# Pooling the second level of keys and values after the projection, on GpSimd, instead of before it

## The chip, the cores and the metric

The kernel runs on one core of a Trainium2 chip. Its engines work side by side, each through its own queue in order: TensorE (PE, with its weight loads as PEld), VectorE (DVE), ScalarE (ACT), GpSimd (POOL), and SyncE (SP), which issues transfers. The metric is device microseconds of one execution. The kernel before takes 3242.17 us, the median of 3 runs from 3239.64 to 3243.61.

## What is computed

The input is `x`, 8 images of 256 channels by 32x32. Three parts follow one another: a pooled attention with a depthwise convolution (layer 0), a self-attention over 1024 positions, and a mixture of 8 experts. The change lies in layer 0 alone, in its keys and values:

```python
kv = jnp.einsum('bchw,oc->bohw', x, kv_w)
k_map, v_map = (kv[:, :C], kv[:, C:])

def pooled(t):
    outs = []
    for i, r in enumerate(POOL_RATIOS):              # [1, 2, 3, 6]
        oh, ow = (round(H / r), round(W / r))        # 32, 16, 11, 5
        Mh, Mw = (_pool_mat(H, oh), _pool_mat(W, ow))
        p = jnp.einsum('bchw,ph,qw->bcpq', t, Mh, Mw)
        p = p + _depthwise(p, dconv_w[i], dconv_b[i])
        outs.append(p.reshape(B, C, -1))
    return jnp.concatenate(outs, axis=2)
```

So the keys and the values each have 1024 + 256 + 121 + 25 = 1426 positions per image: the projected map itself, its means over 2x2 blocks (the second level, 16x16), over blocks of about 3x3 (11x11) and of about 6x6 (5x5), each with a 3x3 depthwise convolution added. Layer norm, scores, softmax and the weighted sum of the values follow. Projection and pooling are both linear, so either may come first.

## The kernel before, in words

`kernel` builds one program. A guarded general version (`layer0_general` and others) follows at its end and runs only if a bound is broken. What is timed is `attention` (layers 0 and 1a, line 913) and `experts`, both written as generators that a planner, `Flow` (line 657), puts into an order while the program is built. Each generator yields the engine that it needs and the tiles that must be ready; `Flow` keeps a clock per engine from modelled costs (`cost`, line 723), the time at which each tile is ready, and, for DVE and POOL, a shared port on which POOL operations and DVE operations with two SBUF inputs follow each other (line 795). Generators have a rank, lower first. `step` (line 882) runs whatever is due between two steps of the main loop, as far as a credit of PE time allows (4.0 us a step for ranks below 5, 2.0 for the others, lines 29 to 31); `finish` runs generators until a condition holds. Every engine's instructions then keep this order on the chip.

**The main loop** (line 1911) goes over 8 batches (images), with 45 steps each: `scores` of one chunk of 128 keys against 512 queries of four heads (four matmuls, then one exp of 128x2048 on ACT, line 1512), and `values` of the chunk before. Pairs of exps are added by accumulating transfers from POOL's queue (`add`, line 1567) and then on DVE (`sums`, line 1574). One PSUM tile `sc` serves all scores, and six `pt` tiles hold the exps.

**Beside it**, for each later batch, `prepare` (line 1381) loads and normalises the image `xi`; `pool_levels` (line 1332) sums its 2x2, 3x3 and 6x6 blocks into `xl`, 402 columns: level 2 on POOL (add neighbouring columns, add neighbouring rows, scale by a quarter), level 3 on POOL, level 4 on DVE. `maps` (line 1114) projects four maps, two channel halves of values (m = 2, 3) and two of keys (m = 0, 1), in the column slices `KEY_SLICES` = 512, 512, 402, the last from `xl`. ACT copies each slice from PSUM to the map `p`, and writes `acc`, the slice times (1 + middle tap) plus the bias, for the levels in that slice. `convolve` (line 1273) adds the eight other taps per level on DVE (`taps`, line 1245), level by level, in `todo`'s order; two buffers `p` and three buffers `acc` limit how far maps run ahead. `by_tokens` turns the result to tokens, normalises it, and `key_tokens` writes the keys `kn`. Once a batch is done with layer 0, the self-attention (`layer1`, `outputs`) of that batch runs in the same gaps of the main loop.

**Batch 0** has its own path, since nothing runs beside it: `first_maps` (line 1173) projects the four maps in another order, and the large level of its keys is convolved on PE with diagonal weights (`first_keys`); `first_taps` does the rest on DVE. The small levels of its two key maps go to a tile `ptail`.

PE's matmuls of 128x128 weights are cut into four column quarters of 32 within the main loop (`Flow.Engine`, line 677), which run beside one another. One fp32 matmul leaves two records in the trace for each piece.

Of the kernel before, what the change touches and what calls it, by code (L numbers as in the profile page):

```python
# [42 lines left out]
LIMIT = 1e12  # L43
KEY_CHUNKS = [(i * P, min(P, NK - i * P)) for i in range(NKC)]
KEY_SLICES = [(0, 512), (512, 512), (1024, 402)]


K_ID, K_GRP, K_ONE, K_S11, K_S5, K_HEAD, K_I32, K_SEL, K_END = 0, 128, 256, 384, 505, 530, 658, 690, 706
# [864 lines left out]
def attention(tc, kit, f, outer, ended, nb, consts, x, t1, t2, hn, bounds, vecs, q_t, kv_t, proj_t, gqk_t, wqk, wqkv, vecs1, w1_d, w1c, gate_d, wrc, vecs2, bnvec):  # L913
# [6 lines left out]
    with ExitStack() as ctx:  # L920
# [50 lines left out]
        def db(c, s):  # L971
# [4 lines left out]
        f.ve.tensor_scalar(  # L976
            mid, vec[:, V_DW : V_DW + 72].rearrange("p (a t) -> p a t", t=9)[:, :, 4], 1.0, None, ALU.add
        )
        hi, lo = bounds
        for t in bounds:  # L980
            f.pool.memset(t, 0.0)
# [119 lines left out]
        def pool(*tiles):  # L1101
            return "POOL", tiles, None
# [4 lines left out]
        def until(cond):  # L1107
            return None, cond, None

        def source(xp, s0, w):  # L1110
            xi, xl = xp
            return xi[:, :, s0 : s0 + w] if s0 < HW else xl[:, :, s0 - HW : s0 - HW + w]

        def maps(xp):

            for m in (2, 3, 0, 1):
                c = m % 2
                yield until(
                    lambda: read[0] >= len(todo) - 1 and len(todo) < (3 + 2 * max(freed[0], 2) if freed[0] else 5)
                )  # L1120
                p = pmaps[len(todo) % 2]
                acc = T(work, [P, NK], "acc", bufs=3)
                for s0, w in KEY_SLICES:
                    if s0 >= HW:
                        yield until(lambda: len(done) >= len(todo) - 1)
                    src = source(xp, s0, w)
                    yield pe(src, tag="sm")
                    ps = small()
                    for k in range(2):
                        f.pe.matmul(  # L1130
                            ps[:, :w],
                            lhsT=kvw[:, k, m * P : (m + 1) * P],
                            rhs=src[:, k, :],
                            start=k == 0,
                            stop=k == 1,
                        )
                    f.act.activation(p[:, s0 : s0 + w], ps[:, :w], AF.Copy)
                    for s, n in enumerate(SIDES):
                        a, z = max(OFFS[s], s0), min(OFFS[s] + n * n, s0 + w)
                        if a < z:  # L1140
                            f.act.activation(
                                acc[:, a:z],
                                ps[:, a - s0 : z - s0],
                                AF.Identity,
                                bias=db(c, s),
                                scale=mid[:, c * 4 + s : c * 4 + s + 1],
                            )
                todo.append((c, p, acc))
# [7 lines left out]
        pmaps = [T(work, [P, NK], f"p{i}") for i in range(2)]  # L1156
        for t in pmaps:
            f.split(t, 512, HW)
        first, large, whole, pooled, asked = {}, [], [], [], []

        def first_diagonals():

# [10 lines left out]
        def first_maps(xp):  # L1173


            for m in range(4):
                if m < 2:
                    p = T(work, [P, 4, 512], "pt", bufs=6).rearrange("p j q -> p (j q)")
                    acc = T(l1, [P, NK], "v") if m else T(work, [P, NK], "kn", bufs=3)
                else:  # L1180
                    p = pmaps[m - 2]
                    acc = T(work, [P, NK], "acc", bufs=3)
                for t in (p, acc):
                    if t is not p or m < 2:
                        f.split(t, 512, HW)
                first[m] = p, acc
            for m, s0 in [(m, s0) for g in (0, 2) for s0 in (0, 512) for m in (g, g + 1)] + [(m, HW) for m in range(4)]:
                if s0 == HW:
                    yield until(lambda: pooled)
                w = min(512, NK - s0)  # L1190
                c = m % 2
                p, acc = first[m]
                src = source(xp, s0, w)
                yield pe(src, tag="sm")
                ps = small()
                for k in range(2):
                    f.pe.matmul(
                        ps[:, :w],
                        lhsT=kvw[:, k, m * P : (m + 1) * P],
                        rhs=src[:, k, :],  # L1200
                        start=k == 0,
                        stop=k == 1,
                    )
                small_levels = s0 == HW and m < 2
                f.act.activation(ptail[:, m, :w] if small_levels else p[:, s0 : s0 + w], ps[:, :w], AF.Copy)
                for s, n in enumerate(SIDES):
                    a, z = max(OFFS[s], s0), min(OFFS[s] + n * n, s0 + w)
                    if a < z and (m >= 2 or s):
                        f.act.activation(
                            acc[:, a:z],  # L1210
                            ps[:, a - s0 : z - s0],
                            AF.Identity,
                            bias=db(c, s),
                            scale=mid[:, c * 4 + s : c * 4 + s + 1],
                        )
                if (m, s0) == (3, 512):
                    large.append("maps")
                    f.spawn(first_keys(0), 1)
                    f.spawn(first_keys(1), 5)
            whole.append("maps")  # L1220
# [38 lines left out]
        def first_taps():  # L1259
            for m in (2, 3):  # L1260
                yield until(lambda: "maps" in large)
                yield from taps(m - 2, 0, *first[m])
                large.append(("values", m))
                read[0] += 1
            yield until(lambda: whole)
            for m in (0, 1, 2, 3):
                p, acc = first[m]
                for s in range(1, 4):
                    yield from taps(m % 2, s, *((ptail[:, m, :], acc, HW) if m < 2 else (p, acc)))
                whole.append(m)  # L1270
            done.extend(first[m][1] for m in (2, 3, 0, 1))

        def convolve():

            for m in range(4, 4 * nb):
                yield until(lambda: len(todo) > m)
                c, p, acc = todo[m]
                for s in range(4):
                    yield from taps(c, s, p, acc)
                    read[0] += s == 0  # L1280
                done.append(acc)
# [50 lines left out]
        def pool_levels(xi, xl):  # L1332
# [2 lines left out]

            def level(s):
                n = SIDES[s]
                return xl[:, :, OFFS[s] - HW : OFFS[s] - HW + n * n].rearrange("p k (h w) -> p k h w", h=n)

            for k in range(2):  # L1340
                one, l2, l3 = img[:, k], level(1)[:, k], level(2)[:, k]

                yield pool(xi)
                t2 = T(work, [P, 32, 16], "pool")
                f.pool.tensor_tensor(t2, one[:, :, 0::2], one[:, :, 1::2], ALU.add)
                yield pool(t2)
                f.pool.tensor_tensor(l2, t2[:, 0::2, :], t2[:, 1::2, :], ALU.add)
                yield pool(t2)
                f.pool.tensor_scalar(l2, l2, 0.25, 1.0, ALU.mult, ALU.mult)

                yield pool(xi)
                t3 = T(work, [P, 32, 11], "pool")
                f.pool.tensor_tensor(t3, one[:, :, 0::3], one[:, :, 1::3], ALU.add)
                yield pool(t3)
                f.pool.tensor_tensor(t3[:, :, 0:10], t3[:, :, 0:10], one[:, :, 2::3], ALU.add)
                yield pool(t3)
                f.pool.tensor_tensor(t3[:, :, 1:11], t3[:, :, 1:11], one[:, :, 2::3], ALU.add)
                yield pool(t3)
                f.pool.tensor_tensor(l3, t3[:, 0::3, :], t3[:, 1::3, :], ALU.add)
                f.pool.tensor_tensor(l3[:, 0:10, :], l3[:, 0:10, :], t3[:, 2::3, :], ALU.add)  # L1360
                yield pool(t3)
                f.pool.tensor_tensor(l3[:, 1:11, :], l3[:, 1:11, :], t3[:, 2::3, :], ALU.add)
                flat = xl[:, k, OFFS[2] - HW : OFFS[3] - HW]
                f.pool.tensor_tensor(flat, flat, con[:, K_S11 : K_S11 + 121], ALU.mult)

            t5 = T(work, [P, 2, 32, 5], "pool")
# [6 lines left out]
            for i, (a, e) in enumerate(ends):  # L1373
                f.ve.tensor_reduce(
                    l5[:, :, i, :], t5[:, :, a:e, :].rearrange("p k h w -> p k w h"), AX.X, ALU.add
                )
            flat = xl[:, :, OFFS[3] - HW :]
            f.ve.tensor_tensor(flat, flat, con[:, None, K_S5 : K_S5 + 25].to_broadcast([P, 2, 25]), ALU.mult)
            pooled.append(True)

        def prepare(b):
# [28 lines left out]
            for k in range(2):  # L1410
# [1 line left out]
                f.ve.tensor_scalar(  # L1412
                    xi[:, k, :], xi[:, k, :], mu[:, k : k + 1], gr[:, k : k + 1], ALU.subtract, ALU.mult
                )
            xl = T(work, [P, 2, NK - HW], "xl")
            if b == 0:
                f.spawn(pool_levels(xi, xl), 2)
            else:
# [1221 lines left out]
```

## Time and profile before

| | |
|---|---|
| median of 3 runs | 3242.17 us |
| the profiled execution | 3241.38 us |
| its span (first to last instruction) | 3239.2 us |
| busy: PE, DVE, ACT, POOL | 3072.6, 2403.2, 1690.1, 1201.7 us |
| mean granted PE clock | 0.985 |
| first scores of batches 0 to 7 | exps from 83, 307, 537, 764, 995, 1219, 1457, 1680 us |
| last exp of the main loop | 1866 us |
| projections of the last slice | 51.9 to 59 us (batch 0), 142 to 1496 us (the others) |
| DVE's taps | 960 instructions into `acc`, 550 us |

The page of a profile gives for each engine its busy time; the stages below it cut the span into windows. A row of a group of instructions reads: line, engine, operation, out<-in, shapes, count, then busy us and mean ns of one, then idle time of the engine just before them and what ended it. All instructions of the planner carry line 670, so groups are told apart by tile names: `sm` and `sx` are PSUM tiles for small work, `p`, `acc`, `xi`, `xl` and `pool` (the sums' scratch tile) are those above.

### The profile page before, as it was taken

The numbers are of one execution on the slowest core, as the hardware profiler recorded it, in microseconds if no ns is written. First come the engines' busy times: TensorE is split into PE (matmuls) and PEld (weight loads), VectorE is DVE, ScalarE is ACT, GpSimd is POOL, SyncE is SP. The second block draws the span as 40 slices with busy tenths as digits, with TensorE's granted clock in tenths as the row PEclk, the third lists the DMA queues.
The fourth block names the chain that finished last, engine by engine and source line by source line (L and its number), as shares of the span: only waits on it lengthen the run. The fifth ranks groups of instructions, "written<-read, shape, count | busy, mean of one in ns | idle before, by whom it ended". The sixth has DMA issues, their size and how long they took to land. (4 is left out here: it accounts for less than half of the span.)

```text
span 3239.2 us, 56567 instructions
## 1 busy us (share of the span) xinstructions
PE 3072.6 (95%) x22678; PEld 1788.4 (55%) x22678; DVE 2403.2 (74%) x4128; ACT 1690.1 (52%) x2302; POOL 1201.7 (37%) x1293
## 2 busy tenths in 40 slices
PE   8787899899999989999999999999999999999998
PEld 3322234343334333433433357777888888888887
DVE  5896888888888888788544545446878788877776
ACT  4675666666666576666655533333333333444443
POOL 2313213223232231321121220006756666777776
PEclk9898999999999999999999999999999999999999
DMA  1467665655656665655667763124344452000000
GB/s 54 93 145 160 123 140 128 145 131 126 160 122 119 158 132 106 163 120 122 145 135 144 156 213 127 59 85 169 140 153 144 148 170 72 20 24 29 20 14 21
DMA packets 117200, 375.54 MB, mean 116 GB/s; under 512 B 14512, under 2 KB 40440, under 8 KB 93696
## 3 DMA queue, kind: packets, MB, share of 16 engines
q0 software_dynamic: 28608, 179.85, 28.6%
q1 hardware_dynamic: 84960, 190.01, 17.3%
q8 instruction: 181, 2.97, 0.4%
q10 hardware_dynamic: 3360, 1.97, 0.2%
q14 instruction: 91, 0.75, 0.1%
HBM read 118.74 MB, written 87.60 MB: 64 GB/s over the span
## 5 line engine op out<-in xcount | busy, mean ns | idle before, releaser
L670 ACT ACTIVATE pt<-sc 128x2048 f32<-128x2048 f32 x352 | 660.7, 1877 | 271.2 <-PE sc L670 222.3
L670 DVE SCALAR_TENSOR_TENSOR acc<-p,vec,acc 128x961 f32<-128x961 f32 (+3 forms) x960 | 550.3, 582 | 31.6 <-ACT acc L670 6.1
L670 PE MATMUL sc<-q,kn 32*128 32x512 f32 (+1 forms) x3072 | 424.1, 653 | 98.5 <-ACT pt L670 94.8
L670 DVE TENSOR_TENSOR pt<-pt,pt 128x1024 f32<-128x1024 f32 x320 | 390.5, 1264 | 162.1 <-DMA pt<-pt 133.9
L670 PE MATMUL pv<-pt,vt 128*32 128x512 f32 x2816 | 388.8, 625 | 2.8 <-ACT vt L670 2.8
L670 ACT ACTIVATE p1c<-bank 128x256 f32<-128x256 f32 x226 | 86.4, 382 | 557.1 <-PE bank L670 545.4
L670 ACT ACTIVATE h<-h,bnvec 128x512 f32<-128x512 f32 x452 | 341.9, 805 | 61.8 <-DVE h L670 53.5
L670 POOL DMA_DIRECT2D pt<-pt x160 | 146.4, 915 | 568.4 <-ACT pt L670 435.1
L670 POOL TENSOR_TENSOR rstd<-rstd,mhalf 128x4 f32<-128x4 f32 (+2 forms) x88 | 102.7, 1168 | 614.4 <-DVE rstd L670 600.6
L670 DVE TENSOR_TENSOR h<-p1c,bank 128x512 f32<-128x512 f32 x226 | 153.9, 681 | 223.6 <-PE bank L670 216.8
L670 PEld LDWEIGHTS sc<-q,kn 32*128 32x128 f32 (+1 forms) x3072 | 114.4, 180 | 293.1 <-ACT pt L670 189.0
L670 POOL TENSOR_TENSOR tm<-h,tm 128x256 f32<-128x256 f32 x202 | 236.2, 1169 | 15.8
L670 DVE TENSOR_TENSOR h<-u,bank 128x256 f32<-128x256 f32 x452 | 230.0, 550 | 7.8
L670 PEld LDWEIGHTS pv<-pt,vt 128*32 128x32 f32 x2816 | 56.3, 109 | 279.0 <-issue 263.5
L670 PE MATMUL bank<-h,w2e 128*128 128x256 f32 (+1 forms) x620 | 204.6, 459 | 2.8 <-DVE h L670 2.0
L670 DVE TENSOR_TENSOR h<-h,gate 128x1024 f32<-128x1024 f32 x128 | 200.3, 1565 | 0.7 <-ACT h L670 0.5
L670 POOL TENSOR_TENSOR tm<-h 128x512 f32<-128x512 f32 x101 | 131.2, 1299 | 187.4 <-ACT h L670 187.4
L670 PE MATMUL sm<-p,v 128*32 128x256 f32 (+1 forms) x2424 | 199.8, 379 | 0.0
L670 PE MATMUL y<-t,s3e 128*128 128x256 f32 x768 | 187.0, 380 | 2.0 <-POOL t L670 2.0
L670 PE MATMUL bank<-t,s1e 128*128 128x256 f32 x750 | 182.5, 379 | 0.2 <-DVE h L670 0.2
L670 POOL TENSOR_TENSOR t<-h 128x512 f32<-128x512 f32 x104 | 135.4, 1302 | 109.2 <-DVE h L670 88.6
L670 PE MATMUL sm<-y,t 128*32 128x256 f32 (+1 forms) x1848 | 169.5, 382 | 5.0 <-DVE res L670 4.1
(315 smaller groups left out, 5453.2 us busy)
## 6 DMA issues: line engine op xcount, KB each, us to landing
pt<-pt POOLq DMA_DIRECT2D x160, 1024.0 KB, 7.7
h<-h SPq DMA_DIRECT2D x142, 512.0 KB
xi<-in_x_dram SPq DMA_DIRECT2D x16, 512.0 KB
t<-t SPq DMA_DIRECT2D x8, 1024.0 KB
res<-t SPq DMA_DIRECT2D x32, 256.0 KB
t<-res SPq DMA_DIRECT2D x32, 256.0 KB
hn<-res SPq DMA_DIRECT2D x32, 256.0 KB
hn<-hn SPq DMA_DIRECT2D x16, 512.0 KB
```

Source lines behind the costliest of these rows:

```text
L670: ins = fn(*args, **kwargs)
```

## The change

The second level of a map is summed by POOL from the projected map `p` and not from the image. The scaling by a quarter is put into the weights of the second level's convolution (and into its middle tap), once, on DVE at the start. The last slice of a projection has 146 columns (levels 3 and 4) where it had 402, and `xl` shrinks with it. A new generator `halve` does the two sums on POOL, and then ACT writes level 2 of `acc` from SBUF instead of from PSUM. It is spawned at rank 1 when a map's last slice is due (batches 1 to 7), and at rank 0 after a map's second slice in batch 0. Level 2's taps wait for it, and so does the start of the map after the next.

```diff
+MAP_SLICES = [(0, 512), (512, 512), (1280, 146)]
...
+        quarter = vec[:, V_DW : V_DW + 72].rearrange("p (c s t) -> p c s t", c=2, s=4)[:, :, 1]
+        f.ve.tensor_scalar(quarter, quarter, 0.25, None, ALU.mult)
+        quarter = mid.rearrange("p (c s) -> p c s", c=2)[:, :, 1]
+        f.ve.tensor_scalar(quarter, quarter, 0.25, None, ALU.mult)
...
+        def halve(p, small_p, c, acc):
+
+            yield pool(p[:, :HW])
+            pm = p[:, :HW].rearrange("p (h w) -> p h w", h=32)
+            t2 = T(work, [P, 32, 16], "pool")
+            f.pool.tensor_tensor(t2, pm[:, :, 0::2], pm[:, :, 1::2], ALU.add)
+            yield pool(t2)
+            l2 = small_p.rearrange("p (h w) -> p h w", h=16)
+            f.pool.tensor_tensor(l2, t2[:, 0::2, :], t2[:, 1::2, :], ALU.add)
+            yield act(small_p)
+            f.act.activation(
+                acc[:, HW : OFFS[2]],
+                small_p,
+                AF.Identity,
+                bias=db(c, 1),
+                scale=mid[:, c * 4 + 1 : c * 4 + 2],
+            )
+            halved.append(acc)
...
-                    lambda: read[0] >= len(todo) - 1 and len(todo) < (3 + 2 * max(freed[0], 2) if freed[0] else 5)
+                    lambda: min(read[0], len(halved)) >= len(todo) - 1 and len(todo) < (3 + 2 * max(freed[0], 2) if freed[0] else 5)
...
-                for s0, w in KEY_SLICES:
+                for s0, w in MAP_SLICES:
                     if s0 >= HW:
                         yield until(lambda: len(done) >= len(todo) - 1)
+                        f.spawn(halve(p, p[:, HW : OFFS[2]], c, acc), 1)
...
+                if s0 == 512:
+                    f.spawn(halve(p, ptail[:, m, :256] if m < 2 else p[:, HW : OFFS[2]], c, acc), 0)
...
                 for s in range(4):
+                    if s == 1:
+                        yield until(lambda: acc in halved)
                     yield from taps(c, s, p, acc)
...
-                one, l2, l3 = img[:, k], level(1)[:, k], level(2)[:, k]
-
-                yield pool(xi)
-                t2 = T(work, [P, 32, 16], "pool")
-                f.pool.tensor_tensor(t2, one[:, :, 0::2], one[:, :, 1::2], ALU.add)
-                yield pool(t2)
-                f.pool.tensor_tensor(l2, t2[:, 0::2, :], t2[:, 1::2, :], ALU.add)
-                yield pool(t2)
-                f.pool.tensor_scalar(l2, l2, 0.25, 1.0, ALU.mult, ALU.mult)
+                one, l3 = img[:, k], level(2)[:, k]
...
-            xl = T(work, [P, 2, NK - HW], "xl")
+            xl = T(work, [P, 2, NK - OFFS[2]], "xl")
```

More of the change, by code (lines that the diff above doesn't have):

```diff
@@ L1111, in source @@
             xi, xl = xp
-            return xi[:, :, s0 : s0 + w] if s0 < HW else xl[:, :, s0 - HW : s0 - HW + w]
+            return xi[:, :, s0 : s0 + w] if s0 < HW else xl[:, :, s0 - OFFS[2] : s0 - OFFS[2] + w]
+        def halve(p, small_p, c, acc):
[15 more added lines that the diff above has]
+            halved.append(acc)
         def maps(xp):
@@ L1158, in attention @@
             f.split(t, 512, HW)
-        first, large, whole, pooled, asked = {}, [], [], [], []
+        first, large, whole, pooled, asked, halved = {}, [], [], [], [], []
         def first_diagonals():
@@ L1189, in first_maps @@
                     yield until(lambda: pooled)
+                    s0 = OFFS[2]
                 w = min(512, NK - s0)
@@ L1203, in first_maps @@
                     )
-                small_levels = s0 == HW and m < 2
-                f.act.activation(ptail[:, m, :w] if small_levels else p[:, s0 : s0 + w], ps[:, :w], AF.Copy)
+                small_levels = s0 > HW and m < 2
+                f.act.activation(
+                    ptail[:, m, s0 - HW : s0 - HW + w] if small_levels else p[:, s0 : s0 + w], ps[:, :w], AF.Copy
+                )
                 for s, n in enumerate(SIDES):
@@ L1278, in convolve @@
                 for s in range(4):
+                    if s == 1:
+                        yield until(lambda: acc in halved)
                     yield from taps(c, s, p, acc)
@@ L1337, in level @@
                 n = SIDES[s]
-                return xl[:, :, OFFS[s] - HW : OFFS[s] - HW + n * n].rearrange("p k (h w) -> p k h w", h=n)
+                return xl[:, :, OFFS[s] - OFFS[2] : OFFS[s] - OFFS[2] + n * n].rearrange("p k (h w) -> p k h w", h=n)
             for k in range(2):
-                one, l2, l3 = img[:, k], level(1)[:, k], level(2)[:, k]
-                yield pool(xi)
-                t2 = T(work, [P, 32, 16], "pool")
-                f.pool.tensor_tensor(t2, one[:, :, 0::2], one[:, :, 1::2], ALU.add)
-                yield pool(t2)
-                f.pool.tensor_tensor(l2, t2[:, 0::2, :], t2[:, 1::2, :], ALU.add)
-                yield pool(t2)
-                f.pool.tensor_scalar(l2, l2, 0.25, 1.0, ALU.mult, ALU.mult)
+                one, l3 = img[:, k], level(2)[:, k]
                 yield pool(xi)
@@ L1362, in pool_levels @@
                 f.pool.tensor_tensor(l3[:, 1:11, :], l3[:, 1:11, :], t3[:, 2::3, :], ALU.add)
-                flat = xl[:, k, OFFS[2] - HW : OFFS[3] - HW]
+                flat = xl[:, k, : OFFS[3] - OFFS[2]]
                 f.pool.tensor_tensor(flat, flat, con[:, K_S11 : K_S11 + 121], ALU.mult)
@@ L1376, in pool_levels @@
                 )
-            flat = xl[:, :, OFFS[3] - HW :]
+            flat = xl[:, :, OFFS[3] - OFFS[2] :]
             f.ve.tensor_tensor(flat, flat, con[:, None, K_S5 : K_S5 + 25].to_broadcast([P, 2, 25]), ALU.mult)
```

## The prediction

> **What bounds the kernel now.** I read the page first (busy time per engine), then the busy time of each engine cut at the starts of the eight batches, because shares over the whole span mix stages.
>
> ```profile
> span 3239.2 us, 56567 instructions
> PE 3072.6 (95%) x22678; PEld 1788.4 (55%) x22678; DVE 2403.2 (74%) x4128; ACT 1690.1 (52%) x2302; POOL 1201.7 (37%) x1293
> ```
>
> PE is busy 95% of the span, so work taken from PE counts wherever PE is what ends last. The stages below (columns: length, then busy us and instructions of PE, PEld, DVE, ACT, POOL, granted clock, DMA) say where that is.
>
> ```profile
> 36.00:80.00 44.00, 41.56 (x131) 21.07 (x129) 36.14 (x74) 16.86 (x37) 5.21 (x8) 1.00 0.09 31
> 80.00:141.00 61.00, 49.06 (x364) 22.67 (x365) 53.38 (x149) 38.91 (x47) 22.01 (x29) 0.86 0.41 88
> 141.00:261.00 120.00, 101.20 (x893) 33.26 (x896) 108.42 (x212) 81.35 (x102) 19.60 (x24) 0.97 0.65 145
> 261.00:307.00 46.00, 33.19 (x204) 9.56 (x204) 21.02 (x40) 25.58 (x25) 12.78 (x15) 0.81 0.66 155
> 307.00:537.00 230.00, 215.09 (x2118) 78.22 (x2114) 183.93 (x345) 152.19 (x187) 74.15 (x85) 0.97 0.62 133
> 764.00:995.00 231.00, 218.96 (x2206) 85.41 (x2198) 197.96 (x364) 149.40 (x187) 62.84 (x72) 0.99 0.63 137
> ```
>
> Two regimes. From 307 us, where batch 1's scores begin, PE is busy 215 of 230 us and DVE 184 to 198: PE decides. The keys agree: their first third is written at 521.7, 712.7, 942.0, 1168.1, 1362.1 and 1566.4 us, and the scores of batches 2 to 7 start at 537, 764, 995, 1219, 1457 and 1680, so the taps run 15 to 114 us ahead of need. In batch 0, from 80 to 261 us, PE is busy 150 of 181 us and DVE 162: there DVE's taps decide, and batch 1's scores start at 307 only 2 us after its keys (304.8).
>
> After 1866 us no map is projected. What runs there (rest of layer 1, experts) is unchanged, and comes earlier or later as a block.
>
> **PE: what is taken away.** Each of 32 maps is projected in slices of 512, 512 and 402 columns; the last becomes 146, so 256 columns go. The rows (columns: busy us, mean ns | idle before):
>
> ```profile
> L670 PE MATMUL sm<-p,v 128*32 128x256 f32 x2080 | 122.6, 379 | 0.0
> L670 PE MATMUL sx<-xl,kvw 128*32 128x402 f32 x160 | 15.4, 501 | 0.0
> L670 PE MATMUL sm<-xi,qw 128*32 128x512 f32 x336 | 39.9, 592 | 0.0
> ```
>
> From 256 to 512 columns a record grows by 592 - 379 = 213 ns, and 402 lies on that line (379 + 146 x 0.832 = 500). The starts of the four column quarters are some 7 ns apart and groups follow each other by the column time, so a map's projection is 2 channel halves x 2 records = 4 such groups: 4 x 213 = 0.85 us a map, 27.3 us in all. By time: 4 maps (3.4 us) between 51.9 and 59.3 us, 4 (3.4 us) between 142 and 229, and 24 (20.4 us) from 340 to 1496, in the PE regime. I count those 20.4 in full and the other 6.8 at nothing, since DVE decides there; their bounds are 0 and -6.8. No row has 146 columns. If the loads of four weight quarters did not hide behind so short a matmul, the spacing could stay at that of 256 columns, 214 ns, instead of 122: then 335 - 214 = 121 ns a group, 24 x 4 x 121 = 11.6 us. I take 122, since 128-column transposes with a load each start 107 ns apart in the timeline.
>
> **POOL: what moves.** Two 128-partition images a batch were summed before projection; now four maps are summed after it.
>
> ```profile
> L670 POOL TENSOR_TENSOR pool<-xi 128x512 f32<-128x512 f32 x16 | 23.8, 1488 | 8.7 <-DVE xi L670 8.7
> L670 POOL TENSOR_TENSOR xl<-pool 128x256 f32<-128x256 f32 x16 | 14.8, 925 | 0.9
> L670 POOL TENSOR_SCALAR xl<-xl 128x256 f32<-128x256 f32 x16 | 10.4, 647 | 1.1
> ```
>
> Gone: 2 x (1.488 + 0.925 + 0.647) = 6.1 us a batch. New: 4 x (1.488 + 0.925) = 9.7. POOL gains 3.5 us a batch, 28 in all; it is busy about 30% in these stages, so the length itself hides.
>
> What need not hide is DVE. Of the 240 taps of 961 or 992 elements on DVE, none overlaps a pooling sum in the records by more than 0.1 us in total; a 10x10 tap that lies wholly inside one is recorded as 0.65 us instead of 0.32. So a pooling sum among taps costs DVE about its own length. The Trainium skill, "SBUF — State Buffer", section "SBUF: two separate sides", says the same more strongly and speaks against this change: VectorE operations with two SBUF inputs and GpSimd operations hold one port pair exclusively, and the loser waits for a whole instruction. By that rule alone all the 13.2 us of the next paragraph are lost; by the rows only what exceeds DVE's idle time is.
>
> In batch 0's stretch (36 to 261 us) eight halvings come in, 8 x 2.41 = 19.3 us, and batch 1's old sums go, 6.1. Batch 0's old sums lie between 14 and 24 us, where DVE waits, and give nothing: the taps start at 36.8 on ScalarE's copy. Net 13.2 us beside a DVE that has 7.9 + 7.6 + 11.6 = 27 us idle there. Bounds 0 and +13.2; I take a third, +4.4, since the first four halvings fall into 36 to 80 us, where the shorter PE chain also lets DVE's own waits shrink. From batch 2 on the extra 3.5 us a batch is covered by the lead of 15 to 114 us: nothing. Without that cover it is 6 x 3.5 = 21 us.
>
> **ACT and the new waits.** The copy shrinks from 402 to 146 columns: (595 - 508) / 110 = 0.79 ns a column, -0.20 us; the level's bias now reads SBUF (about the 592 ns of the token scaling, 256 wide) instead of PSUM (564): +0.03. ACT gets 5.5 us less in all, and is not the bound: nothing. But that activation now waits for POOL, and the exps are queued behind it on ACT, and PE's next scores behind them. A step of the score loop takes some 230 / 45 = 5.1 us, of which scores 1.1 and exp 1.88 are in series, so 2.1 us are spare. The emission order puts the activation where a model expects POOL's 2.4 us to be over; if POOL takes its longest rows instead (3.80 + 1.60), it is 3.0 late, 0.9 over the spare time: 24 x 0.9 = 22 us is the upper bound, 0 the lower. I take 2, because means, not longest rows, are 0.45 and 0.2 above the shortest. The taps of level 2 now wait for that activation too, but eight large taps (8 x 1.24 = 9.9 us) run before them, which covers 2.4 + 0.6. Behind a halving in POOL's queue stand the accumulating transfers (0.9 us each, every 10 us or so); a delay of up to 2.4 us at 4 places a batch meets them rarely: nothing, at most 24 x 2.4 / 10 = 6 us. The two scalings of the weights by a quarter are DVE instructions of 0.17 us in front of the first statistics: +0.3.
>
> **The sum.** -20.4 + 4.4 + 2 + 0.3 = -13.7 us. The profiled execution took 3241.4 us (span 3239.2 and 2.2 around it), 0.8 below the median of 3242.2. 3241.4 - 13.7 = 3227.7, forecast 3228. The order of all instructions is planned from modelled costs, so a change of this kind also reshuffles unrelated work: I allow 10 us below and 7 above for the forecast, 3218 to 3235.
>
> **The rivals.**
> 1. *Everything counts.* DVE's idle time takes the halvings and the first 6.8 us count too: 3241.4 - 27.3 = 3214. For it: PE's 95%. Against it: DVE's 90% from 80 to 261 us.
> 2. *The matmuls do not shorten as their columns do.* At 214 ns a group: -11.6 + 6.7 = 3236.5, no change that can be told.
> 3. *Slower: the lock between POOL and DVE.* Batch 1's keys come the full 13.2 us later, and the taps of later batches stretch by 3.5 each. Batch 2's lead of 15 us shrinks; once the lead is gone PE waits for DVE and its saving is worth nothing: 3241.4 + 13.2 + 0.3 = 3255, and up to 21 more. It decides as soon as a batch's scores start right behind its keys, as batch 1's do now. A longer wait also costs clock: between 261 and 307 us, with PE busy 33 of 46, the granted clock is 0.81. Against it: the leads, and DVE's 14 to 20% idle.
>
> ```profile
> PE sc L670 <- ACT pt L670: 31.3, 20, 6.5
> PE sc L670 <- ACT pt L670: 33.4, 34, 4.5
> ```
>
> These rows (PE's waits from 80 to 310 and from 486 to 1458 us) show the score loop already waiting on exps as much in batch 0 as in four later batches: that is where a delay has no cover.
>
> **How the numbers follow.** A measurement of this kernel can tell about 0.2% (6.5 us) from no change. Forecast 0.42, everything counts 0.15, no change that can be told (rival 2, or losses that eat the gain) 0.16, slower 0.27. Faster by over 0.2%: 0.42 + 0.15 = 0.57; within: 0.16; slower: 0.27. The range takes in rivals 1 and 2 and the first step of rival 3 with part of its second: 3208 to 3262.
>
> **What would show it.** PE's projection of the tail: about 288 ns a record at 146 columns, groups 122 ns apart (rival 2: 214). The start of batch 1's scores: 307 + 4 (rival 3: 320). From there to the last exp, now 307 to 1866: about 20 us shorter, with keys still ahead of every batch. POOL up by 28 us, and ACT's waits for POOL near zero. I am wrong if PE's idle time in batches 2 to 7 grows by more than 10 us, or if the planned order moves work so that the stretch after 1866 us changes length by more than a few us.

## The result and the profile after

The changed kernel takes 3273.85 us, the median of 4 runs from 3269.26 to 3276.09. The kernel before, run beside it, takes 3242.89. The ratio is 1.0101, with a 95% interval of 1.0088 to 1.0114: slower by 1.0%, some 32 us (31 by these medians, 33 by the ratio). The forecast was 3228, with a range up to 3262. The sign is wrong, and the range is missed by 12 us.

The page after, its span and busy time per engine:

```profile
span 3273.4 us, 55709 instructions
PE 3061.8 (94%) x22216; PEld 1796.7 (55%) x22216; DVE 2415.0 (74%) x4130; ACT 1681.6 (51%) x2302; POOL 1229.5 (38%) x1309
```

PE is busy 10.8 us less than before (3072.6), yet the span is 34.2 us longer. So PE's idle time went from 166.6 to 211.6 us, up by 45. The stages, cut where the batches now start (columns as before: length, busy us and instructions of PE, PEld, DVE, ACT, POOL, granted clock, DMA):

```profile
36.00:80.00 44.00, 41.46 (x138) 21.45 (x137) 38.14 (x72) 17.80 (x39) 13.92 (x16) 0.96 0.08 31
80.00:141.00 61.00, 50.43 (x380) 23.52 (x378) 51.16 (x152) 38.42 (x48) 19.68 (x23) 0.86 0.43 95
141.00:261.00 120.00, 95.95 (x815) 32.03 (x815) 108.02 (x196) 77.92 (x96) 24.74 (x28) 0.94 0.63 138
261.00:304.00 43.00, 33.31 (x232) 9.75 (x228) 23.84 (x58) 26.22 (x26) 7.02 (x10) 0.92 0.76 182
304.00:526.00 222.00, 192.29 (x1824) 67.98 (x1820) 172.58 (x316) 142.76 (x173) 61.46 (x69) 0.95 0.62 131
746.00:1007.00 261.00, 233.71 (x2246) 95.59 (x2242) 206.02 (x362) 153.35 (x196) 79.03 (x89) 0.95 0.57 122
```

Batch 0 is not the loss: batch 1's scores start at 304 us, 3 us earlier than before. In batch 1 (the fifth line) PE now idles 30 of 222 us where it idled 15 of 230, and it does 23 us less work (192 us busy, before 215): work that used to fill the gaps was left for later. Batch 3 (the last line) lasts 261 us where it lasted 231. The whole, from the trace:

| batch | 0 | 1 | 2 | 3 | 4 | 5 | 6 | 7 |
|---|---|---|---|---|---|---|---|---|
| its scores start, before | 83 | 307 | 537 | 764 | 995 | 1219 | 1457 | 1680 |
| after | 81 | 304 | 526 | 746 | 1007 | 1248 | 1478 | 1701 |
| PE idle in it, before | 43.5 | 14.9 | 8.8 | 12.0 | 17.7 | 8.8 | 14.3 | 8.2 |
| after | 44.4 | 29.6 | 12.8 | 27.3 | 16.0 | 21.6 | 12.6 | 9.5 |

The last exp of the main loop comes at 1896 us (before: 1866), and what follows it lasts 4 us longer. So the loop lost the time, though the changed kernel was 19 us ahead when batch 3 began.

Batch 3 is longer mostly at its end, where the loop stood for batch 4's keys, `kn` (ACT's last exp of batch 3, the first write of the keys, the first exp of batch 4):

```profile
976.45 1.88 ACT L671 ACTIVATE pt<-sc 128x2048 f32<-128x2048 f32 x1 [0.47 <-PE sc L671]
1004.87 1.09 ACT L671 ACTIVATE kn<-sm 128x512 f32<-128x512 f32 x2 [1.33 <-PE sm L671]
1006.73 1.88 ACT L671 ACTIVATE pt<-sc 128x2048 f32<-128x2048 f32 x1 [0.77 <-PE sc L671]
```

No exp runs for 28.4 us; in the kernel before it was 8.2 us at this place. PE is busy 25.9 of these 28.4 us, with work that the planner takes ahead meanwhile: of the 30 us that batch 3 lasts longer, 15 are work of PE and 15 its idle time, only 2.5 of that in this stand. The keys of batches 2 to 7 now come 11, 9, 2, 12, 46 and 77 us ahead of their scores, where they came 15 to 114 us ahead.

The rows of the change itself (busy us, mean ns of one | idle time before them):

```profile
L671 PE MATMUL sm<-xl,kvw 128*32 128x146 f32 x256 | 10.9, 288 | 0.0
L671 POOL TENSOR_TENSOR pool<-p 128x512 f32<-128x512 f32 x30 | 36.7, 1223 | 166.3 <-ACT p L671 162.1 <-DVE acc L671 4.1
L671 POOL TENSOR_TENSOR p<-pool 128x256 f32<-128x256 f32 x30 | 32.9, 1098 | 6.7 <-DVE acc L671 4.7
L671 ACT ACTIVATE acc<-p,vec,mid 128x256 f32<-128x256 f32 x30 | 18.0, 605 | 11.3 <-POOL p L671 11.1
```

These are as predicted: 288 ns a record at 146 columns, the two sums 2.3 us a map, and ACT's new wait 11 us in all over 30 maps. What grew is another wait, that of the score loop (columns: us in total, times, longest us). Before, over the whole span:

```profile
PE sc L670 <- ACT pt L670: 94.8, 75, 6.5
ACT pt L670 <- DMA pt<-pt: 30.6, 11, 6.0
```

After:

```profile
PE sc L671 <- ACT pt L671: 137.0, 105, 6.0
ACT pt L671 <- DMA pt<-pt: 86.0, 28, 6.7
```

An exp needs one of the six `pt` tiles, and a tile comes free when its accumulating transfer has landed. Those waits went from 30.6 to 86 us, and PE's waits for exps from 95 to 137. One such stretch in the timeline after, ACT's exps (start, length, idle before and its releaser):

```profile
924.36 1.88 ACT L671 ACTIVATE pt<-sc 128x2048 f32<-128x2048 f32 x1 [1.26 <-PE sc L671]
933.54 1.88 ACT L671 ACTIVATE pt<-sc 128x2048 f32<-128x2048 f32 x1 [6.60 <-DMA pt<-pt]
937.63 1.88 ACT L671 ACTIVATE pt<-sc 128x2048 f32<-128x2048 f32 x1 [2.21 <-PE sc L671]
946.00 1.88 ACT L671 ACTIVATE pt<-sc 128x2048 f32<-128x2048 f32 x1 [6.50 <-DMA pt<-pt]
```

and PE's scores in it:

```profile
926.29 1.14 PE L671 MATMUL sc<-q,kn 32*128 32x512 f32 x8
935.47 2.09 PE L671 MATMUL sc<-q,kn 32*128 32x512 f32 x8 [5.75 <-ACT pt L671]
939.56 1.14 PE L671 MATMUL sc<-q,kn 32*128 32x512 f32 x8
947.93 2.09 PE L671 MATMUL sc<-q,kn 32*128 32x512 f32 x8 [5.38 <-ACT pt L671]
```

Score steps had followed each other 3.1 to 4.4 us apart with little other PE work between them, and ran out of free tiles. The wait costs twice: PE stands 5 to 6 us, and the scores behind it take 2.09 us instead of 1.14. The granted clock in these 15 us windows:

```profile
920.00:935.00 15.00, 8.70 (x73) 2.08 (x72) 14.49 (x23) 6.11 (x5) 4.09 (x5) 0.92 0.79 203
935.00:950.00 15.00, 9.02 (x52) 2.02 (x56) 8.53 (x11) 4.17 (x3) 2.84 (x3) 0.73 0.62 132
```

The Trainium skill ("TensorE: Matmul & The Clock Gate", section "What's actually happening") says that the clock halves after some 3.4 us of idleness. The two traces agree: 89 score steps behind waits of 1 to 2 us all took 1.14 us, the 8 behind waits of over 4 us all 2.09, and those behind 2 to 4 us took 1.14 to 2.09. Of the score records of batches 1 to 7, 5.1% are longer than 0.75 us (before: 2.2%). Why steps without filler stand together here is a matter of order, and that is what the experiments separate.

### The profile page after: what moved, and what is told of

It is laid out like the page before. It is cut to its first block, busy times and chain, and to the rows that moved or that the text cites. A ratio compares the mean times of both kernels' runs of the same rounds, so it can differ in the third digit from the quotient of the medians.

```text
span 3273.4 us, 55709 instructions
## 1 busy us (share of the span) xinstructions
PE 3061.8 (94%) x22216; PEld 1796.7 (55%) x22216; DVE 2415.0 (74%) x4130; ACT 1681.6 (51%) x2302; POOL 1229.5 (38%) x1309
## 3 DMA queue, kind: packets, MB, share of 16 engines
q0 software_dynamic: 28608, 179.85, 28.4%
## 5 line engine op out<-in xcount | busy, mean ns | idle before, releaser
L671 DVE SCALAR_TENSOR_TENSOR acc<-p,vec,acc 128x961 f32<-128x961 f32 (+3 forms) x960 | 564.0, 596 | 34.1 <-ACT acc L671 8.3
L671 DVE TENSOR_TENSOR u<-h,bank 128x512 f32<-128x512 f32 x226 | 155.4, 688 | 24.8 <-DVE h L671 0.9
L671 POOL TENSOR_TENSOR t<-h,t 128x256 f32<-128x256 f32 x208 | 166.5, 801 | 16.3
```

Source lines behind the costliest of these rows:

```text
L671: ins = fn(*args, **kwargs)
```

## The experiments

Three theories. **Order**: the planner, fed with other work, puts everything else in another order, and that order costs the 32 us. **GpSimd**: the new sums cost it, by holding up DVE or the transfers in POOL's queue. **Matmul**: PE saved less than it should. Each kernel stands against the kernel before on the same chip (3236.4 to 3240.0 us there).

**Moving the planner's constants.** One constant of the cost model is changed by little, in the old kernel and in the new one. No work is added or taken away. What changes is the order, and with it a few choices that the planner makes by its clocks: which matmuls are cut into quarters (22510 to 22870 PE records in the old orders) and, in six of the twelve runs, which engine does some of the experts' sums (6 or 18 instructions more on POOL). Six constants, with the unmoved pair seven pairs. The edits, in this order: ScalarE's fixed cost (e1 in the old work, e2 in the new), the credit of a step (e9, e8), a tap's fixed cost (e10, e11), GpSimd's fixed cost (e13, e14 pool), the margin by which instructions are held back (e13, e14 margin), and a matmul's cost per column (e15, e16):

```diff
-            return 0.15 + 0.00084 * n + 0.16 * any(i.free_size() == 1 for i in ins[1:])
+            return 0.16 + 0.00084 * n + 0.16 * any(i.free_size() == 1 for i in ins[1:])
...
-PACE1 = 2.0
+PACE1 = 2.1
...
-            return 0.23 + 0.00103 * n
+            return 0.24 + 0.00103 * n
...
-            return 0.15 + (0.0023 if op == "tensor_tensor" else 0.0015) * n
+            return 0.16 + (0.0023 if op == "tensor_tensor" else 0.0015) * n
...
-MARGIN = 1.5
+MARGIN = 1.6
...
-            c = max(0.2, 0.00169 * n)
+            c = max(0.2, 0.00172 * n)
```

> The kernel before, with one constant of the planner's cost model moved: an ACT operation is taken to last 0.16 us + ... instead of 0.15 us + .... No instruction is added or removed, only the order can change. Theory A (the loss comes from what the change adds: the halvings in POOL's queue and the waits on them) expects 3243 within 10 us, since nothing of that is in here. Theory B (the loss is the accident of a new order, any small change of the planner's inputs can cost or give 1%) expects a time that is off by 15 us or more, either way.

> The changed kernel with the same constant moved (ACT 0.16 us + ... instead of 0.15 us + ...). Theory A (the halvings and their waits cost) expects 3274 within 10 us again. Theory B (accident of the order) expects a time that falls anywhere between 3215 and 3280.

> The kernel before with the credit of the low-ranked work raised from 2.0 to 2.1 us a step: a second new order for the work of the kernel before. If the order of the kernel before is a lucky one among its neighbours (theory B in the form: a new order costs whatever it is made for), 3255 or more. If new orders of the old work stay at 3240 within 10 us, as with the ACT constant, the loss belongs to the changed kernel's orders.

> The changed kernel with the credit of the low-ranked work raised from 2.0 to 2.1 us of PE time a step, so that layer 1 may take the 0.08 us a step that the maps leave. If the freed PE time is lost because nothing may fill it (theory D, second half), 3225 to 3250. If any new order falls anywhere (theory B), no relation: 3235 to 3285.

> The kernel before with another constant of the planner moved (a DVE tap taken as 0.24 us + ... instead of 0.23 us + ...): a third order for the old work. As for the run before it: 3255 or more if the old order is a lucky one, 3240 within 10 us if not.

> The changed kernel with the same constant of the taps moved: a fourth order for the new work (3274, 3255 and 3258 so far). If the spread is accident, 3240 to 3275 with no preference; if the changed kernel's own waits in the plan cost, 3250 or more again.

> The kernel before, with the planner's fixed cost of a GpSimd instruction written as 0.16 where it was 0.15; no instruction is added or taken away, only the planned order can differ. Accident of one order: anywhere in 3235 to 3280, and the changed kernel with the same edit falls on either side of it. Systematic (the changed kernel's orders are worse as a kind): 3235 to 3250, with the changed kernel at least 10 us above.

> The changed kernel with the same edit (0.16 for 0.15). Accident: anywhere in 3235 to 3280, as likely below its partner as above. Systematic: at least 10 us above its partner.

> The kernel before, with the planner's margin written as 1.6 where it was 1.5. Accident: 3235 to 3280. Systematic: 3235 to 3250, the partner at least 10 us above.

> The changed kernel with the margin at 1.6. Accident: 3235 to 3280, on either side of its partner. Systematic: at least 10 us above its partner.

> The kernel before, with the planner's cost of a matmul column written as 0.00172 where it was 0.00169; only the planned order can differ. Accident of one order: 3235 to 3280. Systematic: 3235 to 3265, the changed kernel with the same edit at least 10 us above.

> The changed kernel with the same edit (0.00172 for 0.00169). Accident: 3235 to 3295, on either side of its partner. Systematic: at least 10 us above its partner.

Medians in us, the ratio to the kernel before with its interval, and PE's idle time in batch 1 and in all in the profiled execution:

| constant | old work | ratio | idle | new work | ratio | idle | new - old |
|---|---|---|---|---|---|---|---|
| unmoved | 3242.2 | 1 | 14.9, 167 | 3273.9 | 1.0101 (1.0088 to 1.0114) | 29.6, 212 | +31.7 |
| ScalarE | 3238.0 | 0.9996 (0.9985 to 1.0007) | 20.0, 171 | 3254.7 | 1.0048 (1.0031 to 1.0064) | 25.0, 200 | +16.7 |
| pace | 3243.7 | 1.0014 (1.0003 to 1.0024) | 17.8, 177 | 3257.7 | 1.0055 (1.0038 to 1.0072) | 30.4, 197 | +14.0 |
| tap | 3275.0 | 1.0105 (1.0086 to 1.0123) | 22.8, 197 | 3272.4 | 1.0103 (1.0086 to 1.0120) | 32.7, 209 | -2.6 |
| GpSimd | 3263.2 | 1.0083 (1.0066 to 1.0100) | 20.3, 186 | 3292.4 | 1.0167 (1.0150 to 1.0184) | 26.9, 222 | +29.2 |
| margin | 3265.2 | 1.0095 (1.0075 to 1.0115) | 16.1, 187 | 3260.6 | 1.0070 (1.0053 to 1.0087) | 28.1, 207 | -4.5 |
| matmul | 3275.8 | 1.0125 (1.0108 to 1.0142) | 18.7, 197 | 3253.7 | 1.0049 (1.0029 to 1.0068) | 23.9, 190 | -22.1 |

The old work alone covers 3238 to 3276 us by its order, the new work 3254 to 3292. One order against another is worth as much as the whole result. Two of the six moved old orders (e1, e9) stayed within 5 us of the unmoved one, the four others cost 21 to 34 us. These four lost it mostly elsewhere than the changed kernel: their last exps come at 1860 to 1876 us (before: 1866), and what follows takes 1395 to 1406 us (before: 1372), with PE busy 10 to 14 us more in it. In the changed kernel the last exp comes at 1896, and 1376 us follow.

The mean of the seven pairs is +8.9 us with a standard error of 7.4 (worked out from the last column). So neither "each new order is worse by 10" nor "no difference as a kind" is borne out by the times. The pairs are not quite independent: the GpSimd pair's new order has the same stand of 28 us before batch 4 as the changed kernel, which none of the other five new orders has, and these two pairs have the largest differences, +31.7 and +29.2. Two quantities do separate the kinds, however. PE's idle time in batch 1 is larger in all seven pairs, by 5 to 15 us, 9.4 in the mean (over the whole execution it is larger in six of the seven, by 22 in the mean). And the transfers `pt<-pt` are issued later: the time from the end of a pair's second exp to the issue of its transfer, summed over 160 of them, is 305 to 338 us in the seven old orders and 359 to 425 in the seven new ones, 323 and 392 in the mean.

How a halving makes a transfer late is seen in the trace after. Nine transfers were issued late right behind a halving, 75 us in sum, between 1.7 and 8.2 us each but for one of 30.0 in batch 0. One of them, on POOL:

```profile
565.43 0.88 POOL L671 DMA_DIRECT2D t<-xr  x1 [0.34 <-ACT xr L671]
573.23 1.68 POOL L671 TENSOR_TENSOR pool<-p 128x512 f32<-128x512 f32 x1 [6.92 <-ACT p L671]
574.98 1.57 POOL L671 TENSOR_TENSOR p<-pool 128x256 f32<-128x256 f32 x1
576.49 0.89 POOL L671 DMA_DIRECT2D pt<-pt  x1
```

The exp that this transfer waits for had ended at 569.4. POOL was idle then, but the halving stood at the head of its queue and waited 6.9 us for ACT's copy of the map. The transfer behind it left 7.1 us late. But these nine are a small part of the rise: counted in order, the same nine transfers were 56 us late in the kernel before (this one 6.1, the one of 30.0 was 25.2), six of them behind other instructions of POOL. And the rise does not explain the time by itself. In e3 and e4 below the sum is 323 and 329 us, as in the old orders; yet PE idles 27.1 and 23.6 us in batch 1, as in the new ones, and e4 is as slow as the changed kernel.

**The old order held, 256 columns taken away (e5).** The planner is told the old costs, so that the order stays; the matmuls of the last slice run on 146 columns, and nothing else of the change is in (level 2 gets other columns of the same size).

```diff
+            n = 402 if n == 146 else n
...
+                    o = 256 if s0 == HW else 0
...
-                            ps[:, :w],
+                            ps[:, o:w],
...
-                            rhs=src[:, k, :],
+                            rhs=src[:, k, o:w],
```

> The kernel before in its own order, instruction by instruction: only the last slice's matmuls have 146 columns instead of 402, while the planner is told the cost of 402. POOL sums before the projection as in the kernel before; level 2 is left without its own values (ScalarE copies other columns of the same size). This is the PE saving alone, 27.3 us of PE time, with no new order. Theory B (the saving is real, the new order loses it) expects 3242 - 15 to 27 = 3215 to 3227. Theory D (PE is not what sets the pace in the score loop: its steps wait on exps and transfers, and PE work taken away turns into idle time) expects 3235 to 3245.

**The new order held: sums one element long (e6), and 256 columns put back (e7).** `told` is the cost that the planner is given in place of its own: the full sums' in e6, none in e7, so that the order stays.

```diff
-            f.pool.tensor_tensor(t2, pm[:, :, 0::2], pm[:, :, 1::2], ALU.add)
+            f.told = 0.15 + 0.0023 * 512
+            f.pool.tensor_tensor(t2[:, 0, 0:1], pm[:, 0, 0:1], pm[:, 16, 0:1], ALU.add)
+            f.told = None
...
-            f.pool.tensor_tensor(l2, t2[:, 0::2, :], t2[:, 1::2, :], ALU.add)
+            f.told = 0.15 + 0.0023 * 256
+            f.pool.tensor_tensor(l2[:, 0, 0:1], t2[:, 0, 0:1], t2[:, 0, 0:1], ALU.add)
+            f.told = None
```

```diff
+                    if s0 > HW:
+                        f.told = 0.0
+                        for k in range(2):
+                            f.pe.matmul(
+                                ps[:, 146:402],
+                                lhsT=kvw[:, k, m * P : (m + 1) * P],
+                                rhs=kvw[:, k, :256],
+                                start=True,
+                                stop=True,
+                            )
```

> The changed kernel in its own order, instruction by instruction, but the two sums of a halving take one element instead of 512 and 256, while the planner is told their full cost. Level 2 is left without its values. Theory A (the sums and the port that POOL shares with DVE cost 30 us) expects 3235 to 3250. Theories B and D expect 3262 to 3276, since the order and PE's work are the same.

> The changed kernel in its own order, with the 256 columns that the change took from PE put back (an unused product of 256 columns behind each last slice, which the planner counts as nothing): PE has the work of the kernel before again. If PE sets the pace in this order, 3274 + 20 to 27 = 3294 to 3301. Theory D (PE waits anyway) expects 3272 to 3284.

**The whole change in the old order (e12).** Everything that the change computes, with its sums, its level 2 from SBUF and the quarter in the weights, but planned with the old costs. The new instructions are issued `silent`, that is without the planner's clocks moving, so that all others keep their places; the sums have a scratch tile of their own, and level 2's activation is placed by hand behind four taps of level 1.

```diff
+        def halve(p, small_p):
+            f.silent = True
...
+            t2 = T(work, [P, 32, 16], "half")
```

> The whole change, computing everything, inside the order of the kernel before: PE, DVE and SP have its order exactly (two scalings of weights on DVE apart); the planner is told the old costs, POOL's halvings stand behind each map's last slice, and ScalarE's level-2 activation behind the fourth large tap. If the order is what lost (theory B), the PE saving of 15 us at this order comes out, less the sums' cost of 8 at the other order, plus what the old sums no longer take: 3222 to 3238. If the new waits (POOL behind ScalarE's copies, ScalarE behind POOL) are what loses, 3245 or more.

| kernel | order | what it does | median us | ratio to before (interval) | PE busy, idle |
|---|---|---|---|---|---|
| before | old | old work | 3242.2 | 1 | 3072.6, 166.6 |
| e5 | old | old, 146 columns | 3224.7 | 0.9953 (0.9937 to 0.9970) | 3053.8, 174.6 |
| e12 | old | the whole change | 3235.5 | 0.9988 (0.9978 to 0.9997) | 3051.3, 181.2 |
| after | new | the whole change | 3273.9 | 1.0101 (1.0088 to 1.0114) | 3061.8, 211.6 |
| e6 | new | sums of one element | 3265.6 | 1.0082 (1.0066 to 1.0099) | 3060.6, 203.8 |
| e7 | new | 256 columns put back | 3296.7 | 1.0181 (1.0164 to 1.0198) | 3087.9, 205.2 |

The page of e12 and its batches 1 and 3, against 192 of 222 and 234 of 261 us in the rows after:

```profile
span 3232.5 us, 56591 instructions
PE 3051.3 (94%) x22678; PEld 1785.5 (55%) x22678; DVE 2416.8 (75%) x4130; ACT 1681.0 (52%) x2302; POOL 1221.9 (38%) x1309
```

```profile
309.00:536.00 227.00, 209.10 (x2106) 77.81 (x2098) 183.95 (x346) 150.75 (x188) 67.60 (x78) 0.97 0.62 134
761.00:987.00 226.00, 212.86 (x2190) 84.37 (x2186) 196.72 (x359) 147.70 (x185) 67.08 (x75) 0.98 0.64 140
```

and its waits in the score loop:

```profile
PE sc L671 <- ACT pt L671: 96.3, 82, 6.5
ACT pt L671 <- DMA pt<-pt: 23.3, 10, 6.2
```

The page of e6, and its two sums (busy us, mean ns):

```profile
PE 3060.6 (94%) x22216; PEld 1795.4 (55%) x22216; DVE 2392.6 (73%) x4130; ACT 1683.3 (52%) x2302; POOL 1183.5 (36%) x1312
L671 POOL TENSOR_TENSOR pool<-p 128x1 f32<-128x1 f32 x30 | 10.3, 344 | 177.4 <-ACT p L671 177.4
L671 POOL TENSOR_TENSOR p<-pool 128x1 f32<-128x1 f32 x30 | 15.0, 501 | 2.3
```

What follows. The matmul theory falls: the columns are worth 0.47% (15 us) in the old order, and putting them back costs 0.8% (23 us by the medians) in the new one. The GpSimd theory explains a small part: e6, with the sums' length gone, is 6 to 8 us faster (0.19% by the ratios, about the joint width of their intervals); e12 above e5 is 0.35% (11 us) for the sums with all the new waits. The same change that costs 1.0% in the new order gains 0.12% in the old one. The rest, 1.0101 / 0.9988 = 1.0113 or some 37 us, is the order, the places of the new instructions in it included. One other thing is in these 37 us: in e12 the sums have a scratch tile of their own, in the changed kernel they share one with the query projections and the other levels. No run holds the new order and changes the tile alone. The trace after shows little of it: it puts the halvings' waits down to ACT's copy (162 of 166 us), and ACT's waits at that tile are 12.9 us (before: 4.6).

**Two more edits at the sums (e3, e4).** e3 gives the sums a scratch tile of their own; e4 leaves the sums out and writes zeros into level 2 once. Both let the planner make a new order.

```diff
-            t2 = T(work, [P, 32, 16], "pool")
+            t2 = T(work, [P, 32, 16], "half")
```

```diff
-            f.pool.tensor_tensor(t2, pm[:, :, 0::2], pm[:, :, 1::2], ALU.add)
...
-            f.pool.tensor_tensor(l2, t2[:, 0::2, :], t2[:, 1::2, :], ALU.add)
-            yield act(small_p)
+            yield act(p[:, :HW], small_p)
...
+            f.pool.memset(t[:, HW : OFFS[2]], 0.0)
```

> The changed kernel, with the scratch tile of the halving as a tile of its own instead of the one that the query projections, the third and the fourth level share. If that sharing makes queries, the next image's load and so the keys of batch 4 late (theory C: the chain from map to map is what grew), the time falls to 3235 to 3255 and batch 4's scores no longer start right behind its keys. If the halvings hurt by their place in POOL's queue, ahead of the accumulating transfers (theory A), it stays at 3265 to 3280.

> The changed kernel without the two sums of a halving (level 2 stays at zero, everything else is computed): 64 POOL operations less, and ScalarE's level-2 activation waits only for the map. Theory A (sums and waits in POOL's queue) expects the PE saving to come out: 3242 - 20 to 27 = 3215 to 3225. Theory B (accident of the order) expects no relation: anything from 3215 to 3280. A third (the narrow projections themselves cost, for example by moving PE's work to where it idles) expects 3255 or more.

e3 takes 3256.8 us (ratio 1.0044, 1.0027 to 1.0061), e4 3274.5 (1.0101, 1.0084 to 1.0118). Leaving out all of POOL's new work changes nothing, and a scratch tile of its own gains 17 us. As each makes a new order, and orders alone spread over 38 us, neither says anything of the sums by itself. In e3 batch 4's keys come early again (the loop stands 1.9 us before batch 4), as was expected of a conflict on the scratch tile, and the time is 2 us above the range expected of it; but five of the seven new orders have no such stand either, with the tile shared, so e3 does not show that conflict. e3 also shows a trap: its last exp comes at 1844 us, 52 earlier than after, but the experts' gate, which needs layer 1 finished, only at 2237, since more of layer 1 was left behind the loop (in the changed kernel: 1896 and 2239).

## Why the prediction was wrong

**The failed step** is the last one of the sum: "a change of this kind also reshuffles unrelated work: I allow 10 us below and 7 above". The seven old orders spread over 38 us, and the step from the old order to the new one cost some 37 with the change in both. With it fell the cover that the sum counted on: the keys' lead of 15 to 114 us was taken as given, but it belongs to the old order. It is 14 to 113 us in e12, and 2 to 77 us in the new order, where the loop stood 28 us for batch 4's keys. The allowance was a guess without a row behind it, and it was the largest unknown of the case. Nothing in the profile of before could show it. But the score loop's waits for exps, 95 us in all, showed that the order does not hide them everywhere, so that another order could make them more or fewer, and the range had to be wide on both sides. "I am wrong if PE's idle time in batches 2 to 7 grows by more than 10 us" named the sign: it grew from 69.8 to 99.8. Even at a fixed order the sum was too good, -4 us (e12) where it said -13.7: PE's saving gave 15 and not 20.4, and the rest took 11 and not 6.7.

**PE's saving** (27.3 us in all, 20.4 counted) was right in mechanism, and near in size. A record takes 288 ns, and groups start 122 to 128 ns apart (456.97, 457.09, 457.22, 457.35 us in the trace after; before 437.21, 437.55). So rival 2, 214 ns, falls. PE's busy time falls by 18.8 us when the columns are taken away in the old order (e5), and rises by 26.1 us when they are put back in the new one (3087.9 - 3061.8). In time they gave 15 us in the old order (10 to 20 by the interval) and 23 in the new. That PE's busy time fell only 10.8 us is no failure of this term: other PE work became 8 to 15 us dearer in the new order (18.8 or 26.1, less 10.8), the records at the lower clock among it.

**The halvings beside DVE** (4.4 us, bounds 0 to 13.2) **and the new waits** (2, bounds 0 to 22) and the weights (0.3), 6.7 together, measured 11 in the old order (e12 against e5, some 6 either way by the intervals), within their bounds. Batch 1's scores start at 309 us in e12, 2 later than before, where 4 were expected. With sums of one element DVE's records are 22 us shorter in all (2392.6 against 2415.0), so a pooling sum does lengthen DVE's work. It does so by half of the 44 us by which those sums shrink (69.6 to 25.3 us), and in the old order (e12 against e5) by 14.4 us for 21.1 us more of POOL's work: the Trainium skill's rule of a whole lost instruction ("SBUF — State Buffer", "SBUF: two separate sides") is the upper bound here and not the value, and 6 to 8 us of it reach the end. The row that the prediction read for this is not in the trace: 10x10 taps that overlap a pooling sum are recorded there as 0.44 to 1.03 us, none of them as 0.65.

**Transfers behind a halving** ("nothing, at most 24 x 2.4 / 10 = 6 us") left something out: the step counted the halving's own 2.4 us and not its wait for ACT's copy, which stands in the same queue (162 us of POOL's idle time in the row above). The lateness of the transfers rose by 83 us in this kernel, of which the nine behind halvings make 19 (75 against 56), and by 69 in the mean of the seven pairs. What that costs in time has not been isolated: e12 has the same sums, in places where the transfers' lateness sums to 327 us (before: 309), and e6, whose sums are short but stand in the new places, has 382.

**Rival 3** (the lock, keys late, 3255 and more) had the right side for another reason. Keys did become late, batch 4's being written at 1004.9 us with its scores at 1007, which was its sign. But the lock is not the cause: batch 1's keys came early, the stand before batch 4 is 28.0 us with sums of one element too (e6), without the sums (e4) batch 4's scores start 2 us behind its keys again and the time is the same, and with the full sums in the old order (e12) the leads stay.

**What stays open.** The 32 us divide into the change itself, -4 us at a fixed order, and the order, +37. How much of that is this one pair's accident and how much belongs to the new orders as a kind is settled only roughly: the pairs' mean of +8.9 (7.4) less -4 leaves some 13 us with the kind and some 23 with the pair, each with 7 or more of uncertainty. The unmoved old order is one of the three good ones of its seven. What in the new orders makes batch 1 idle is not known: late transfers alone are not it, as e3 and e4 show. What the stand before batch 4 cost is not isolated either, since PE worked through most of it; that the two orders with it have the largest differences of the seven is no proof.

## What to carry to other kernels

Where a planner or scheduler orders the whole program from modelled costs, a change has two prices: the work's, read from rows, and the new order's, which no row shows. Price the second one by moving a constant of the model in the unchanged kernel a few times, and judge the change itself with the order held. A lead that covers a delay belongs to the order in which it was read; after a new order, read it again. Into an in-order queue, a new instruction brings its wait as well as its length: ask what stands behind it while it waits.

## What the runs showed of the hardware

Waits of 5.4 and 5.75 us on PE were followed by eight score records in 2.09 us instead of 1.14; the wait's price on PE is about 1 us more for each such step. Behind waits of 1 to 2 us the scores kept their 1.14 us (89 steps in the traces before and after). Groups of four column quarters of 146 columns, with 128 rows of weights each, follow each other at 122 to 128 ns, so that the loads of their weights hide behind so short a matmul too. GpSimd sums beside DVE's work lengthened DVE's records by half of their own length in one pair of runs (22 of 44 us, e6 against after) and by two thirds in another (14.4 of 21.1, e12 against e5).
